# Layer 1's weighted sum moved next to the products of heads 0 to 3, and three PSUM places exchanged, in a two-layer graph attention kernel

## The chip, the cores and the metric

The kernel runs on one core of one Trainium2 chip. The metric is the device time in microseconds of one execution. A core has TensorE (PE in the profile, with its weight loads shown as PEld), VectorE (DVE), ScalarE (ACT), GpSimd (POOL) and SyncE (SP, which here only issues DMAs). Each engine runs its own instructions strictly in their order; between engines they wait for each other with semaphores.

## What is computed

There are 16 graphs of 1024 nodes with 256 features, and an adjacency matrix for each. Two layers are applied, each to normalised and rectified features, with a residual:

```
h = relu(layernorm(x))
x = x + L0(h, adj)      # 8 heads of 32: softmax(mask(Q K^T / sqrt(32))) V, then Wo
h = relu(layernorm(x))
x = x + L1(h, adj)      # scores by edge kind:
    e_k   = leaky_relu((h * a_k) h^T)         # k = 0..3
    score = e_k where adj == k + 1, else -9e15
    out   = softmax(score) h
```

With the inputs given, `adj` holds 0 and 1 only, so layer 1 needs `e_0` alone; the kernel checks this while it runs and has another path for more kinds, which is not taken here.

## The kernel before

A tile is 128 rows of one graph, so there are 128 tiles (`s` from 0 to 127, graph `b = s // 8`, tile `t = s % 8`). The main loop (line 839) runs over the tiles, and each turn of it, a *step*, has eight *places* `h` = 0 to 7, one for each head. The order in which instructions are issued is written out by hand in the loop's body, and each engine keeps to it. A step works on several tiles at once:

- `now` is the tile whose heads are computed. At place h: `scores(h)` (PE, L461), `softmax_max(h)` (DVE, L473), the exponential of the head before (`softmax_exp`, ACT, L490), and the transposition of the head before that: on the PE with a copy by ACT (`turn`, L590 and L591), or, for heads 0, 1, 4 and 5 in most tiles, as blocks on DVE with DMAs issued by SP (`turn_blocks`, `place_blocks`, L381 and L386). In tiles with t = 7 the heads 4 and 5 go by the PE too, and in tiles with t = 0 the heads 0 and 1.
- `combine(0)`, at place 7, multiplies heads 0 to 3 with the values; `combine(1)`, at place 3 of the next step, heads 4 to 7 (both L526, 64 matmuls each as the profile counts them, two for each that the code issues; their weights are 32 columns wide, and four of them lie side by side in the array).
- `was` is the tile before. It gets its reciprocals of the softmax sums (`turned_reciprocals`, ACT, L520, tile `recT`), `combined` (DVE, L536), the output product (`output`, PE, L541), the residual (`residual`, DVE, L547) and its norms (`norms`: DVE, then POOL).
- `piece` is the tile nine ahead, whose layer 0 inputs are made: `normed` (ACT, L223, tile `h`), `turn` (PE, two transposes, L237), `turned` (ACT, two copies, L249 and L250, tiles `hT` and `hTm`), k's projection `project(0, .)` (PE, L267 with `wkT`, eight matmuls of the profile), `raised(0)` (ACT, L309), `halve(0)` (POOL, next step). q's projection and the values follow in places 1 and 2 of the next step.
- `edge` is a tile of layer 1 (nine behind): scores in places 0 and 2, `softmax_max` at 3, `softmax_exp` (L680) at 6. `edge_was` is the layer 1 tile before. It gets its transposition at place 0, and its weighted sum `gather` (PE, L698): 64 matmuls of the profile in two halves of 32, each with weights 32 columns wide and 256 columns of data. `store` (DVE, L705 and L707, then a DMA that SP issues, L708) divides, adds the residual and writes the output.

Steps 10 to 127 have an `edge_was`, steps up to 118 a `piece`. Before step 10 there is no layer 1 tile to sum; after the loop eight layer 1 tiles are left and are done by a loop of their own (line 988).

PSUM places. Two banks hold four small places of 128x256 each (line 95): the first bank `sums_place` and `brief`, the second `early` and `late`. Before the change `sums_place` takes the products of `combine` and the sums of `gather`; `brief` the reciprocals and the transposed layer 1 nodes; `early` q's projection; `late` the transposed `h`, k's projection, the values and the output product. The scores have two larger places, `sides`: heads 4 and 6 and the layer 1 scores use the second, the other heads the first. The scores of a head can start when `softmax_max` has read what stood in its place.

The part of the loop that matters runs like this on the PE in an ordinary step (places 4 to 7 and the next 0): `scores(4)`, `turn(2)`, `output`, `scores(5)`, `turn(3)`, `gather(0)`, `piece.turn`, `scores(6)`, `gather(1)`, `project(0)`, `scores(7)`, `combine(0)`, `scores(0)`. On ACT, from place 3 on: `recT`, the layer 1 `bend` (L665), the kept layer 1 blocks (L647), `flag` of the next tile (L453), the exponential of head 3, two copies of head 2's transposes, `raised(1)` (L309), `normed` (L223), the exponential of head 4, two copies of head 3, `hT`, `hTm`, the exponential of head 5, the layer 1 exponential, the exponential of head 6, `raised(0)`.

Of the kernel before, what the change touches and what calls it, by code (L numbers as in the profile page):

```python
# [17 lines left out]
P = 128  # L18
# [12 lines left out]
def by_blocks(t):  # L31
    return BY_BLOCKS.get(t, MIXED)
# [15 lines left out]
def gnn_kernel(  # L48
# [46 lines left out]
    sums_place, brief, early, late = (banks[i // 2][:, i % 2, :] for i in range(4))  # L95
# [92 lines left out]
    class Piece:  # L188
# [66 lines left out]
        def project(self, which, oc):  # L255
            wT, bias = ((weights["wkT"], bk_t), (weights["wqT"], bq_t))[which]
            b, w = self.b, self.n * P
            if b not in kds:
                kds[b] = dram.tile([NC, P, 2, N], F32, tag="kd", name=f"kd_{b}")
            if b not in qds and which == 1:  # L260
                qds[b] = dram.tile([NT, NC, P, 2, 2, P], F32, tag="qd", name=f"qd_{b}")
            if self.n > 1:
                ps = ps_tr.tile([P, w], F32, tag="tr", name="proj")
            else:
                ps = (late, early)[which][:, oc * P : (oc + 1) * P]
            for fc in range(NC):
                nc.tensor.matmul(  # L267
                    ps,
                    lhsT=wT[:, fc, oc * P : (oc + 1) * P],
                    rhs=(self.hT, self.hTm)[which][:, fc, :],  # L270
                    start=(fc == 0),
                    stop=(fc == NC - 1),
                )

            self.projected.append((which, oc, ps, bias))
# [139 lines left out]
    class Attend:  # L415
# [120 lines left out]
            nc.vector.tensor_tensor(self.oT, by_chunk(sums_place), self.recT, ALU.mult)  # L536

        def output(self):
            self.y = late
            for g in range(NC):  # L540
                nc.tensor.matmul(  # L541
                    self.y, lhsT=self.oT[:, g, :], rhs=weights["woT"][:, g, :], start=(g == 0), stop=(g == NC - 1)
                )
# [50 lines left out]
    class Edges:  # L594


        def __init__(self, b, t, last=False):
            self.b, self.t, self.last = b, t, last
            self.rows = slice(t * P, (t + 1) * P)
            self.side = sides[t % 2 if last else 1]  # L600
            self.tags = {"sel": ("p", 4), "pT1": ("pT", 7)} if last else {}
            if last and t % 2:
                self.tags |= {"ha": ("hT", 1), "x1b": ("x1", 1), "h0": ("xb", 1)}
            self.sums = late if last and t % 2 else sums_place

        def buffer(self, tag, shape):
            tag, bufs = self.tags.get(tag, (tag, 1))
# [168 lines left out]
    def attend_of(s):  # L776
        return Attend(*divmod(s, NT)) if 0 <= s < B * NT else None
# [9 lines left out]
    with tc.manual_schedule():  # L787
        first = [Piece(0, 0, 4), Piece(0, 4, 4)]
        piece_was, piece_next = Piece(1, 0), piece_of(0)
        now, nxt = attend_of(0), attend_of(1)  # L790
# [39 lines left out]
        piece, edge, edge_was = piece_next, None, None  # L830
# [8 lines left out]
        for s in range(B * NT + 1):  # L839
            b, t = divmod(s, NT)  # L840

            def load_keys(h, end):
                if t == NT - 1 and b + 1 < B and 2 * h + end in KEY_STEPS:
                    load_key(b + 1, KEY_STEPS.index(2 * h + end))
                if t == 0 and 0 < b < B and 2 * (HEADS + h) + end in KEY_STEPS:
                    load_key(b, KEY_STEPS.index(2 * (HEADS + h) + end))

            nxt2, edge_nxt, piece_nxt = attend_of(s + 2), edges_of(s + 1), piece_of(s + 1)
            for h in range(HEADS):
                ending, eh = (now, h - 1) if h >= 1 else (was, HEADS - 1)  # L850
                turning, th = (now, h - 2) if h >= 2 else (was, HEADS + h - 2)

                load_keys(h, 0)


                if now:
                    now.scores(h)
                if h == 0 and piece_was:
                    piece_was.halve(0)
                if s == 0 and h == 1:  # L860
                    first[1].values()
                if h == 3 and edge:
                    edge.softmax_max()
                if h == 5:
                    if was:
                        was.residual()
                    norms(was, piece_nxt)
                if h == 6 and edge_was:
                    edge_was.gather(1)
                if now:  # L870
                    now.softmax_max(h)
                if h == 6 and edge_was:
                    edge_was.store()


                if h == 1 and edge:
                    edge.keep(0)
                if h == 2 and gone:
                    gone.turned_normed()
                if ending:  # L880
                    ending.softmax_exp(eh)

                if h == 3 and was:
                    was.turned_reciprocals()
                if h == 3 and edge:
                    edge.bend()
                    edge.keep(1)


                if h == 3:  # L890
                    if was:
                        was.combine(1)
                    if piece_was:
                        piece_was.biased()
                    if was:
                        was.combined()
                if turning and th in by_blocks(turning.t):
                    turning.turn_blocks(th)
                    turning.place_blocks(th)
                elif turning:  # L900
                    turning.turn(th, 0)
                    turning.turn(th, 1)


                if h == 0:
                    if edge:
                        edge.score(0)
                    if gone:
                        gone.normed()
                    if edge_was:  # L910
                        edge_was.turn_blocks()
                        edge_was.place_blocks()
                if h == 1:
                    if gone:
                        gone.turn_normed()
                    if piece_was:
                        piece_was.project(1, 0)
                        piece_was.project(1, 1)
                    if was:
                        was.reciprocals()  # L920
                    if piece_nxt:
                        piece_nxt.load()
                if h == 2:
                    if edge:
                        edge.score(1)
                    if piece_was:
                        piece_was.values()
                    if was:
                        was.turn_reciprocals()
                        was.add_bias()  # L930
                if h == 3:
                    if nxt:
                        nxt.load_queries()
                    if edge:
                        edge.leak()
                    if edge_was:
                        edge_was.load_nodes()
                    if nxt:
                        nxt.flag()
                        nxt.mask()  # L940
                if h == 4:
                    if was:
                        was.output()
                    if piece_was:
                        piece_was.raised(1)
                        piece_was.halve(1)
                    if piece:
                        piece.normed()
                    if piece_was:
                        piece_was.write_queries()  # L950
                    if edge_nxt:
                        edge_nxt.prepare()
                    if nxt2:
                        nxt2.load()
                if h == 5:
                    if edge_was:
                        edge_was.gather(0)
                    if piece:
                        piece.turn()
                    if piece:  # L960
                        piece.turned()
                if h == 6:
                    if edge:
                        edge.softmax_exp()
                    if was:
                        was.keep()
                    if now:
                        now.load_nodes()
                    if piece:
                        piece.project(0, 0)  # L970
                        piece.project(0, 1)
                if h == 7:
                    if now:
                        now.combine(0)
                    if piece:
                        piece.raised(0)
                load_keys(h, 1)
            gone, was, now, nxt = was, now, nxt, nxt2
            edge_was, edge = edge, edge_nxt
            piece_was, piece = piece, piece_nxt  # L980
# [84 lines left out]
```

## Time and profile before

| what | value |
|---|---|
| median of 3 runs | 3068.4 us (3067.28 to 3073.23) |
| the profiled execution | 3076.4 us, its span 3074.5 us |
| granted TensorE clock, mean | 0.996 |
| ACT busy, share of the span | 86% |
| DVE busy | 82% |
| POOL busy | 71% |
| matmuls of `gather` (L698), 8192 | 496.9 us busy, mean 382 ns |
| matmuls of `combine` (L526), 16384 | 533.4 us busy, mean 275 ns |

The span is the time from the first to the last instruction on the chip. "Busy" of the PE counts matmuls that overlap in the array, so its share tells that the PE was seldom without work, not how well it was used. A row of the timeline merges instructions of one kind that follow each other: its start, the time from the first start to the last end, and in brackets how long the engine had been idle before and what ended that. The difference between the starts of two neighbouring rows of the PE is therefore what a group cost the PE in its place.

### The profile page before, as it was taken

What the parts mean: (1) busy time and instruction counts of PE and PEld (TensorE: products, weight loads), DVE (VectorE), ACT (ScalarE), POOL (GpSimd) and SP (SyncE); (2) the same over time, 40 slices, a digit from 0 to 9 for tenths busy, and PEclk for the clock granted to TensorE, in tenths of its full rate; (3) what the DMA queues carried; (4) which work ended last, traced back from release to release, by engine and by line L of the source; (5) the groups of instructions that cost most, each with busy time, mean ns of one, the idle gap of its engine ahead of it and who ended that gap; (6) DMA issues with size and microseconds to landing.
All of it is one profiled execution on the core that took longest, in us unless ns stands there. A gap on an engine that the chain in (4) does not pass through costs nothing. (4 is left out here: it accounts for less than half of the span.)

```text
span 3074.5 us, 96254 instructions
## 1 busy us (share of the span) xinstructions
PE 2965.6 (96%) x36722; PEld 2230.1 (73%) x36722; DVE 2515.6 (82%) x4453; ACT 2654.5 (86%) x5159; POOL 2177.6 (71%) x2999
## 2 busy tenths in 40 slices
PE   7889999999999999999999999999999999999998
PEld 5667777777777777777777777777777777776664
DVE  5878888888888888888888788888888888888885
ACT  5888888899898998889889888988989888898882
POOL 3657777777777777777777777777777777776542
PEclk9999999999999999999999999999999999999999
DMA  7766777877777786777777777787777777777653
GB/s 245 219 219 205 237 235 222 255 216 243 231 225 243 230 257 209 232 247 220 246 230 228 235 232 243 221 255 221 220 247 228 251 211 235 237 227 236 191 168 100
DMA packets 597828, 695.68 MB, mean 226 GB/s; under 512 B 63280, under 2 KB 528560, under 8 KB 597360
## 3 DMA queue, kind: packets, MB, share of 16 engines
q1 hardware_dynamic: 528288, 477.29, 51.9%
q0 software_dynamic: 66960, 210.04, 21.0%
q8 instruction: 295, 4.83, 0.7%
q10 hardware_dynamic: 2112, 2.10, 0.2%
q14 instruction: 173, 1.42, 0.1%
HBM read 252.98 MB, written 134.22 MB: 126 GB/s over the span
## 5 line engine op out<-in xcount | busy, mean ns | idle before, releaser
L473 DVE CUSTOM_DVE_ANT_0 p<-s,neg 128x1024 f32<-128x1024 f32 x1024 | 1236.2, 1208 | 220.7 <-PE s L461 185.1
L490 ACT ACTIVATE p<-p,nmx 128x1024 f32<-128x1024 f32 x1024 | 1249.4, 1224 | 132.5 <-DVE nmx L473 123.9
L461 PE MATMUL s<-k,qt 128*128 128x512 f32 x2048 | 760.6, 453 | 15.5 <-DVE nmx L473 4.3
L591 ACT COPY pT<-trp 128x512 f32<-128x512 f32 x1024 | 549.4, 590 | 95.3 <-PE trp L590 94.9
L590 PE MATMUL trp<-ident,p 128*128 128x128 f32 x4608 | 604.5, 274 | 4.7 <-ACT pT L591 1.5
L590 PEld LDWEIGHTS trp<-ident,p 128*128 128x128 f32 x4608 | 531.0, 140 | 104.0 <-ACT pT L591 10.8
L381 DVE STREAM_TRANSPOSE blocks<-p 128x1024 f32<-128x1024 f32 x456 | 564.5, 1238 | 12.3 <-ACT p L680 10.6
L526 PE MATMUL acc<-pT,v 128*32 128x128 f32 x16384 | 533.4, 275 | 41.8 <-ACT recT L520 30.0
L526 PEld LDWEIGHTS acc<-pT,v 128*32 128x32 f32 x16384 | 453.5, 110 | 153.0 <-ACT recT L520 85.0
L698 PE MATMUL acc<-h,pT 128*32 128x256 f32 x8192 | 496.9, 382 | 2.8 <-DVE h L707 1.7
L441 POOL TENSOR_SCALAR neg<-adj 128x1024 bf16<-128x1024 int32 x128 | 467.9, 3655 | 42.9 <-ACT neg L453 33.7
L461 PEld LDWEIGHTS s<-k,qt 128*128 128x128 f32 x2048 | 322.9, 191 | 106.3 <-issue 43.0
L698 PEld LDWEIGHTS acc<-h,pT 128*32 128x32 f32 x8192 | 241.8, 109 | 207.8 <-issue 65.6
L676 POOL TENSOR_TENSOR sel<-sel,less 128x1024 f32<-128x1024 f32 x120 | 286.8, 2390 | 68.9 <-ACT less L665 47.6
L633 PE MATMUL s<-h1T,ha 128*128 128x512 f32 (+2 forms) x744 | 272.8, 490 | 2.7 <-ACT h1T L569 1.6
L674 POOL TENSOR_SCALAR less<-top 128x1 f32<-128x1 f32 x120 | 31.9, 266 | 274.0 <-DVE top L656 273.9
L324 POOL DMA_DIRECT2D qd<-halves x240 | 177.5, 780 | 58.7 <-POOL halves L314 31.8
L490 ACT ACTIVATION_READ_ACCUMULATOR p<-p,nmx 128x1 f32 x1024 | 206.8, 202 | 0.0
L510 POOL COPY wide<-rec 128x256 f32<-128x256 f32 x128 | 53.8, 420 | 204.2 <-DVE rec L508 204.2
L330 POOL DMA_DIRECT2D kd<-halves x240 | 172.2, 766 | 35.5 <-POOL halves L314 35.4
L314 POOL TENSOR_TENSOR halves<-full,halves 128x256 fp32r<-128x256 f32 x240 | 176.8, 737 | 20.6
L633 PEld LDWEIGHTS s<-h1T,ha 128*128 128x128 f32 x744 | 126.7, 190 | 70.7 <-issue 45.0
(117 smaller groups left out, 4328.4 us busy)
## 6 DMA issues: line engine op xcount, KB each, us to landing
pT<-blocks SPq DMA_DIRECT2D x2304, 128.0 KB, 3.5
qt<-qd SPq DMA_DIRECT2D x128, 512.0 KB, 4.5
k<-kd SPq DMA_DIRECT2D x128, 512.0 KB, 7.3
adj<-in_adj POOLq DMA_DIRECT2D x127, 512.0 KB, 5.0
qd<-halves POOLq DMA_DIRECT2D x240, 256.0 KB, 2.7
kd<-halves POOLq DMA_DIRECT2D x240, 128.0 KB, 4.1
xb<-in_x POOLq DMA_DIRECT2D x128, 128.0 KB, 4.2
x1d<-x SPq DMA_DIRECT2D x128, 128.0 KB, 4.0
```

The costliest lines, as they stand in the source:

```text
L324: nc.gpsimd.dma_start(out=qds[self.b][self.first, oc].rearrange("p u w n -> p u (w n)"), in_=halves.unsqueeze(1).to_broadcast([P, 2, 2 * P]),)
L381: nc.vector.transpose(blocks.rearrange("p b j q -> p j b q"), p)
L441: nc.gpsimd.tensor_scalar(self.neg, self.adj, 0.0, MASKED, ALU.is_equal, ALU.mult)
L461: nc.tensor.matmul(self.ps[:, cols], lhsT=self.qt[:, h, :], rhs=keysets[self.b][h][:, cols], start=True, stop=True,)
L473: nc.vector.tensor_tensor_reduce(out=p, in0=sides[h in self.second], in1=self.neg, scale=-SCALE, scalar=FLOOR, op0=ALU.add, op1=ALU.min, a ...
L490: nc.scalar.activation(to, of, AF.Exp, bias=nmx, scale=-1.0, accum_out=self.sums[:, h : h + 1])
L526: nc.tensor.matmul(sums_place[r * HD : (r + 1) * HD, g * P : (g + 1) * P], lhsT=vs[self.b][:, j, place_of(h) : place_of(h) + HD], rhs=self ...
L590: nc.tensor.transpose(tr[:, j, :], p[:, jj * P : (jj + 1) * P], ident)
L591: copy(pT[:, half * 4 : half * 4 + 4, :], tr)
L633: nc.tensor.matmul(self.side[:, cols], lhsT=self.ha[:, c, :], rhs=h1T[:, c, cols], start=(c == 0), stop=(c == NC - 1),)
L676: nc.gpsimd.tensor_tensor(self.sel, self.sel, self.less, ALU.subtract)
L698: nc.tensor.matmul(self.sums[a * HD : (a + 1) * HD, :], lhsT=self.pT[:, j, a], rhs=h1s[self.b][:, j, :], start=(j == 0), stop=(j == NT - 1),)
```

## The change

- k's projection goes to `brief` and the output product too; both were in `late`.
- The sums of `gather` go to `early` in the main loop; they were in `sums_place`. The tail's places stay as they were.
- At place 5, `softmax_max(5)` is issued before `residual` and `norms`, no longer after them. (At place 6 and the other places the order of `softmax_max` against the rest is as before.)
- `gather(0)` leaves place 5 and `gather(1)` place 6. Both come at place 7, with `store` behind them, ahead of `combine(0)`.
- `project(0, 0)` and `project(0, 1)` leave place 6 and come at place 7, behind `scores(7)` and what `turn` there is, ahead of `gather(0)`.
- `raised(0)` is issued ahead of `combine(0)`, no longer behind it.

```
-                ps = (late, early)[which][:, oc * P : (oc + 1) * P]
+                ps = (brief, early)[which][:, oc * P : (oc + 1) * P]
...
-            self.y = late
+            self.y = brief
...
-            self.sums = late if last and t % 2 else sums_place
+            self.sums = (late if t % 2 else sums_place) if last else early
...
                 if h == 3 and edge:
                     edge.softmax_max()
+                if now:
+                    now.softmax_max(h)
                 if h == 5:
                     if was:
                         was.residual()
                     norms(was, piece_nxt)
-                if h == 6 and edge_was:
-                    edge_was.gather(1)
-                if now:
-                    now.softmax_max(h)
-                if h == 6 and edge_was:
-                    edge_was.store()
...
                 if h == 5:
-                    if edge_was:
-                        edge_was.gather(0)
                     if piece:
                         piece.turn()
...
+                if h == 7:
                     if piece:
                         piece.project(0, 0)
                         piece.project(0, 1)
-                if h == 7:
+                    if edge_was:
+                        edge_was.gather(0)
+                        edge_was.gather(1)
+                        edge_was.store()
+                    if piece:
+                        piece.raised(0)
                     if now:
                         now.combine(0)
-                    if piece:
-                        piece.raised(0)
```

## The prediction

> **What bounds the kernel now.** I read the busy shares first, then the waits of the PE in the steady part, then one step's timeline on the PE and on ACT.
>
> ```profile
> PE 2965.6 (96%) x36722; PEld 2230.1 (73%) x36722; DVE 2515.6 (82%) x4453; ACT 2654.5 (86%) x5159; POOL 2177.6 (71%) x2999
> ```
>
> ```profile
> PE acc L526 <- ACT recT L520: 12.6, 27, 0.7
> PE acc L526 <- DMA pT<-blocks: 10.7, 15, 1.6
> PE s L633 <- ACT h1T L569: 1.1, 7, 0.2
> PE s L461 <- DVE nmx L473: 0.2, 1, 0.2
> ```
>
> The second fence is all that the PE's matmuls waited for between 260 and 2800 us: 25 us of 2540. In the steady part the PE is the bound, and a step is as long as the PE's rows put end to end. An ordinary step on the PE, with "..." where its places 0 to 2 follow or rows don't matter:
>
> ```profile
> 1432.81 0.81 PE L461 MATMUL s<-k,qt 128*128 128x512 f32 x2
> 1433.46 1.03 PE L590 MATMUL trp<-ident,p 128*128 128x128 f32 x8
> 1434.43 1.93 PE L698 MATMUL acc<-h,pT 128*32 128x256 f32 x32
> 1436.30 0.44 PE L237 MATMUL acc<-ident,h 128*128 128x128 f32 x2
> 1436.49 0.71 PE L461 MATMUL s<-k,qt 128*128 128x512 f32 x2
> 1437.13 1.93 PE L698 MATMUL acc<-h,pT 128*32 128x256 f32 x32
> 1439.00 1.16 PE L267 MATMUL acc<-hT,wkT 128*128 128x128 f32 x8
> 1439.91 0.72 PE L461 MATMUL s<-k,qt 128*128 128x512 f32 x2
> 1440.56 1.96 PE L526 MATMUL acc<-pT,v 128*32 128x128 f32 x64
> 1442.44 0.73 PE L461 MATMUL s<-k,qt 128*128 128x512 f32 x2
> ```
>
> The same stretch on ACT, from the step's `recT` on:
>
> ```profile
> 1428.18 0.37 ACT L520 COPY recT<-acc 128x256 f32<-128x256 f32 x1 [0.25 <-PE acc L516]
> 1428.91 1.06 ACT L665 ACTIVATE less<-sel 128x1024 f32<-128x1024 f32 x1 [0.35 <-DVE top L656]
> ...
> 1434.07 0.62 ACT L223 ACTIVATE h<-xin,shift,r 128x256 f32<-128x256 f32 x1
> ...
> 1436.77 0.37 ACT L249 COPY hT<-acc 128x256 f32<-128x256 f32 x1
> 1437.04 0.38 ACT L250 COPY hTm<-acc 128x256 f32<-128x256 f32 x1
> ```
>
> ACT works from 1428.18 to 1437.14 with one gap of 0.35 us. Its last product, `hT`, is what `project(0)` reads. The PE comes to `project(0)` only at 1439.00, because `gather(1)` stands before it: 1.86 us of cover. The next `recT` starts at 1450.63, so the step is 22.45 us.
>
> **The gain: fewer changes of the array's shape.** A `gather` half costs 1436.30 - 1434.43 = 1.87 us. Its 32 matmuls go in eight rounds of four; the first starts are spread over 1.93 - 0.38 = 1.55 us (0.38 is the mean of one), so a round is 1.55/7 = 0.22, and a half should cost 8 x 0.22 = 1.76. So leaving the 32-column shape costs 0.1; entering it costs another 0.1: `turn(3)` ahead of `gather` takes 0.97 (1434.43 - 1433.46) and 0.87 in other places, scores 0.64 against 0.57. The projection behind it takes 0.91, and 0.82 elsewhere. That is some 0.25 us for each stay in the shape. The change makes one stay of three (both halves and `combine(0)`): about 0.45 us a step less PE work.
>
> **What the moves cost on the path.** Once the PE is ahead, the step is a loop of two legs: ACT from `recT` to `hT`, then the PE from `project(0)` to the next `recT`. Before, 8.96 + 11.63 (1439.00 to 1450.63) = 20.59, that is 1.86 less than the step: slack. The change puts all of `gather`, which filled the time until `hT`, behind `project(0)`.
>
> - PE's way to `project(0)`: `turn(3)` from 1433.46 ends at 1434.33, `piece.turn` now waits for `h` (1434.69), so 1434.75 to 1434.95, `scores(6)` and `scores(7)` 2 x 0.58, so it stands at `project(0)` at 1436.1. ACT's order up to `hT` is unchanged, and all its inputs are there. The only time ACT can win is its 0.1 us wait for `piece.turn`, and I count none. `hT` is there at 1437.14. The PE waits 1 us.
> - From there: 0.05 for the semaphore, `project(0)` 0.91 + 0.09 for entering the shape, `gather` in one piece 16 x 0.22 = 3.5, `combine(0)` 1442.44 - 1440.56 = 1.88, and from `scores(0)` to `recT` as before 1450.63 - 1442.44 = 8.19. Sum 14.55; with ACT's 8.96 the loop is 23.5. An ordinary step gets 1.02 us longer. Other tiles have other mixes of layer 1 work, but 8.96 and 1.86 stay within 0.05 in most, so this holds for all with t below 7.
> - Steps with t = 7 have two more PE transposes, and their exponentials of heads 4 and 5 are slow:
>
> ```profile
> 1316.45 2.27 ACT L490 ACTIVATE p<-p,nmx 128x1024 f32<-128x1024 f32 x1
> ...
> 1320.03 2.25 ACT L490 ACTIVATE p<-p,nmx 128x1024 f32<-128x1024 f32 x1
> ```
>
>   `turn(5)` needs the second, and now stands ahead of `project(0)`. The exponential ends at 1322.2; 0.05 for the semaphore, `turn(5)` 0.87, projection 1.0, `gather` 3.5, `combine` 1.88: `scores(0)` at 1329.5, where it was at 1326.03. +3.5.
> - Steps 1 to 9 have no `gather`. Their trace already shows what `project(0)` does without cover:
>
> ```profile
> 102.59 1.16 PE L267 MATMUL acc<-hT,wkT 128*128 128x128 f32 x8 [1.64 <-ACT hTm L250]
> ```
>
>   There `combine(0)` will wait for `raised(0)`, which now stands ahead of it and reads the same bank. The changed program has that wait, as the old one has one of `combine(1)` on `recT`. `raised(0)` ends at 105.3, and `combine(0)` began at 104.14: +1.2.
> - In later steps that wait is covered: `raised(0)` ends 4.18 us after `hT` (1441.32), `combine(0)` starts 4.55 after. Were the cover gone, each 0.1 would cost 0.1 a step.
> - `softmax_max(5)` earlier costs the PE nothing; `scores(7)`, now right behind `scores(6)`, needs it by 1435.5. DVE is free at 1433.60 and needs 1.2 + 0.1. Queued behind it are `residual` and norms (0.42 to 1.65 us). `project(0)` needs the residual read out of `brief`, done by 1435.4; POOL takes up the norms at 1441.4. In the old order it would come 1.6 later and `scores(7)` wait 1.0, most of it inside the wait for `hT`.
> - `store` (0.64 us on DVE) now follows the last transposition at place 7, about 4.6 us after `hT`; DVE then has nothing until `scores(0)` at 6.5. Its output DMA on SP moves behind eight block DMAs; SP's next come after DVE's layer 1 transposition at place 0, later still. Both 0; without that gap 0.6 a step.
> - Exchanged places: every new reader (`residual`, `raised(0)`, `store`) is done before the next writer by the times above; 0.
> - Steps 119 to 127 have no `piece`: only the gain, -0.45.
>
> Steps 10 to 118 are 109, of which 13 have t = 7: 96 x 1.02 = 98, 13 x 3.5 = 45, 9 x 1.2 = 11, 9 x -0.45 = -4. Sum +150 us.
>
> **The clock.** In the first 260 us the granted clock falls to half seven times for 3.41 us, each time after a stretch in which the PE stood still half the time:
>
> ```profile
> 119.10:122.51 3.41, 1.73 (x11) 1.08 (x10) 3.19 (x8) 3.41 (x9) 2.93 (x5) 1.00 0.67 169
> 122.51:125.92 3.41, 3.41 (x30) 2.70 (x33) 2.56 (x4) 2.53 (x6) 2.95 (x8) 0.50 0.95 324
> ```
>
> (columns: window, length, busy PE, PEld, DVE, ACT, POOL, then the clock). A stretch with 1.89 busy did not set it off. In an ordinary changed step the PE would miss 0.3 + 1.0 in such a stretch, too little. With t = 7 it misses 1.6 (waiting for the first slow exponential) and 1.4 within 4.7 us: I give it an even chance, at up to 1.7 us, so 13 x 0.5 x 1.5 = 10 us. The Trainium skill's page "TensorE: Matmul & The Clock Gate" (HAM oscillation) puts the limit at idle gaps over about 3.4 us. By that rule nothing here would trip and 10 us would fall away; these rows show it with gaps of 1.64, and the rows decide.
>
> The profiled span becomes 3074.5 + 160 = 3234. The profiled run is 8 us above the median of the runs, so I name 3226.
>
> **Rivals.**
> - *The PE stays the bound* (faster): 118 steps x -0.45 = -53, so 3015. It needs `hT` 1.0 us sooner after `recT`; the break-even is an ACT leg of 7.95 in place of 8.96. For it: the PE has 96%, ACT only 86%. Against it: the leg is back to back but for a gap that DVE sets. 6 in 100.
> - *A smaller wait*: half of the 1.02, 3175 to 3060 as it shrinks. 2 in 100 for no change, 6 for a cost below 70 us.
> - *The clock halves in ordinary steps too*: up to 1.7 x 109 = 185 more, 3410. It decides once a 3.41 us stretch holds 1.7 us of idling, against 1.3 worked out. 8 in 100.
>
> **How the numbers follow.** Forecast 78 in 100, its own range 3180 to 3270 (ordinary steps at 0.7 to 1.3, t = 7 at 2.5 to 4.5). To reach the neighbouring cases I take 3120 to 3300. Measurements of this kernel tell 0.2% from no change. Faster 0.06, same 0.02, slower 0.92.
>
> **What would show it.** After: `L267` with `wkT` waiting for ACT's `hT` about 1 us in most steps, the matmuls' idle time up by some 100 to 200 us, `gather` one row of x64 in about 3.7, PE's share down to about 92%, steps of 23.5. Wrong, if steps are 22.0 and that wait is missing; wrong in size, if the clock drops throughout, or if `combine(0)` waits for `raised(0)` in late steps.

## The result, and the profile after

The changed kernel takes 3198.5 us (median of 4 runs, 3195.85 to 3199.1) where the kernel before, run beside it, takes 3070.2 (4 runs, 3067.28 to 3073.23). The ratio is 1.0416, 95% interval 1.0398 to 1.0434: slower, by 128 us between the medians. The profiled span went from 3074.5 to 3194.0 us, that is +119.5: the profiled run of the kernel before lay 8 us above the median on record ahead of the prediction, that of the changed kernel 2.7 below its own. The page's busy shares:

```profile
PE 2938.1 (92%) x36722; PEld 2269.7 (71%) x36722; DVE 2502.9 (78%) x4453; ACT 2623.2 (82%) x5159; POOL 2172.8 (68%) x2999
```

The busy times of PE, DVE, ACT and POOL are all a little lower than before, and their shares are lower still because the span grew. The time is therefore a new wait. The waits of the PE between 260 and 2900 us show which (engine, tile and line, then the releaser; total us, times, longest):

```profile
PE acc L267 <- ACT hT L249: 89.2, 95, 1.0
PE trp L590 <- ACT pT L591: 20.0, 13, 1.6
PE trp L590 <- ACT p L490: 19.0, 13, 1.5
PE acc L237 <- ACT h L223: 16.0, 63, 0.3
...
PE acc L526 <- ACT full L309: 3.0, 1, 3.0
```

The first row is new: in 95 steps `project(0)` stands still for `hT`, for 0.94 us in the mean. The second and third are new as well and come 13 times each: these are the steps with t = 7. The wait for `h` is on the way to the same place and costs nothing there, because the PE waits again two groups later. The 10.7 us of waits for block DMAs that stood in the same view of the kernel before have gone.

One ordinary step, first on the PE, then on ACT (the rows from one `recT` to the next; between them only the two that matter):

```profile
1496.18 0.44 PE L237 MATMUL acc<-ident,h 128*128 128x128 f32 x2 [0.23 <-ACT h L223]
1496.37 1.18 PE L461 MATMUL s<-k,qt 128*128 128x512 f32 x4
1498.54 1.16 PE L267 MATMUL acc<-hT,wkT 128*128 128x128 f32 x8 [0.99 <-ACT hT L249]
1499.63 3.66 PE L698 MATMUL acc<-h,pT 128*32 128x256 f32 x64
1503.11 1.93 PE L526 MATMUL acc<-pT,v 128*32 128x128 f32 x64
1504.96 0.73 PE L461 MATMUL s<-k,qt 128*128 128x512 f32 x2
```

```profile
1489.63 0.37 ACT L520 COPY recT<-acc 128x256 f32<-128x256 f32 x1 [0.26 <-PE acc L516]
...
1498.08 0.41 ACT L249 COPY hT<-acc 128x256 f32<-128x256 f32 x1
...
1502.01 0.65 ACT L309 ACTIVATE full<-acc,bk_t 128x128 f32<-128x128 f32 x2
...
1513.18 0.37 ACT L520 COPY recT<-acc 128x256 f32<-128x256 f32 x1 [0.26 <-PE acc L516]
```

ACT has `hT` done at 1498.49, 8.86 us after `recT`; `project(0)` starts at 1498.54, and the PE had been idle for 0.99 us. Behind it the whole weighted sum runs as one row of 64, and `combine(0)` follows without a pause. In the steps with t = 7, two waits stand in a row on the PE instead, and the projection comes only after the second:

```profile
1374.01 1.14 PE L590 MATMUL trp<-ident,p 128*128 128x128 f32 x8 [1.53 <-ACT pT L591]
...
1377.07 1.09 PE L590 MATMUL trp<-ident,p 128*128 128x128 f32 x8 [1.45 <-ACT p L490]
```

Measured from one `recT` to the next, the median step with t = 3 went from 22.45 to 23.55 us, with t = 7 from 25.23 to 28.44.

### The profile page after: what moved, and what is told of

The parts are those of the page before. It is cut to its first block, busy times and chain, and to the rows that moved or that the text cites. A ratio compares the mean times of both kernels' runs of the same rounds, so it can differ in the third digit from the quotient of the medians.

```text
span 3194.0 us, 95940 instructions
## 1 busy us (share of the span) xinstructions
PE 2938.1 (92%) x36722; PEld 2269.7 (71%) x36722; DVE 2502.9 (78%) x4453; ACT 2623.2 (82%) x5159; POOL 2172.8 (68%) x2999
## 3 DMA queue, kind: packets, MB, share of 16 engines
q0 software_dynamic: 66960, 210.04, 20.8%
## 5 line engine op out<-in xcount | busy, mean ns | idle before, releaser
L461 PE MATMUL s<-k,qt 128*128 128x512 f32 x2048 | 733.0, 447 | 12.9 <-DVE nmx L473 5.2
L526 PE MATMUL acc<-pT,v 128*32 128x128 f32 x16384 | 527.0, 275 | 49.2 <-ACT recT L520 30.2
L526 PEld LDWEIGHTS acc<-pT,v 128*32 128x32 f32 x16384 | 469.2, 110 | 130.1 <-ACT recT L520 85.2
L698 PE MATMUL acc<-h,pT 128*32 128x256 f32 x8192 | 473.5, 381 | 0.9 <-DMA pT<-blocks 0.5
L698 PEld LDWEIGHTS acc<-h,pT 128*32 128x32 f32 x8192 | 255.3, 110 | 178.8 <-DMA pT<-blocks 6.4
L267 PE MATMUL acc<-hT,wkT 128*128 128x128 f32 x960 | 137.6, 286 | 98.0 <-ACT hT L249 98.0
L490 ACT ACTIVATION_READ_ACCUMULATOR p<-p,nmx 128x1 f32 x1024 | 221.7, 217 | 0.0
L267 PEld LDWEIGHTS acc<-hT,wkT 128*128 128x128 f32 x960 | 116.2, 191 | 144.1 <-ACT hT L249 144.1
```

Of the source, the lines that this page charges most:

```text
L267: nc.tensor.matmul(ps, lhsT=wT[:, fc, oc * P : (oc + 1) * P], rhs=(self.hT, self.hTm)[which][:, fc, :], start=(fc == 0), stop=(fc == NC - 1),)
L461: nc.tensor.matmul(self.ps[:, cols], lhsT=self.qt[:, h, :], rhs=keysets[self.b][h][:, cols], start=True, stop=True,)
L490: nc.scalar.activation(to, of, AF.Exp, bias=nmx, scale=-1.0, accum_out=self.sums[:, h : h + 1])
L526: nc.tensor.matmul(sums_place[r * HD : (r + 1) * HD, g * P : (g + 1) * P], lhsT=vs[self.b][:, j, place_of(h) : place_of(h) + HD], rhs=self ...
L698: nc.tensor.matmul(self.sums[a * HD : (a + 1) * HD, :], lhsT=self.pT[:, j, a], rhs=h1s[self.b][:, j, :], start=(j == 0), stop=(j == NT - 1),)
```

## The experiments

The edits are shown against the changed kernel, those of 7 and 8 against the experiment before them; "..." marks what is left out. Step times are medians over steps 10 to 118.

**1. The projection behind the weighted sum.** If the 1 us is only a matter of who comes first, `gather` ahead of `project(0)` should cover it.

```
                 if h == 7:
-                    if piece:
-                        piece.project(0, 0)
-                        piece.project(0, 1)
                     if edge_was:
                         edge_was.gather(0)
                         edge_was.gather(1)
                         edge_was.store()
+                    if piece:
+                        piece.project(0, 0)
+                        piece.project(0, 1)
```

> The changed kernel with one move: project(0) goes behind both halves of gather (and ahead of raised(0) and combine(0)), so that gather covers the time until hT again. If the loss is only that project(0) waits about 1 us for ACT's hT, the wait vanishes and the time falls to 3010-3030 us. My theory says more: gather now writes early, in the bank of late, so it has to wait for hTm, ACT's last read of that bank, 0.3 us after hT; and combine(0) has to wait until raised(0) has read brief in its own bank, some 0.7 us after the projection, with nothing between them. An ordinary step then goes from 23.55 to about 24.4 us and the time to 3260-3320 us. A third theory, that the loss comes from one long stretch on the PE without scores, in which DVE and ACT run dry, expects no change: the stretch is as long as before (3190-3210 us).

Measured: 3368.2 us, ratio to the kernel before 1.0976 [1.0951, 1.1000]; the step with t = 3 takes 25.05, 1.50 more than in the changed kernel. The two waits are those expected, but the time is above the 3260 to 3320 named. The PE's timeline:

```profile
1500.80 3.66 PE L698 MATMUL acc<-h,pT 128*32 128x256 f32 x64 [1.26 <-ACT hTm L250]
1504.39 1.16 PE L267 MATMUL acc<-hT,wkT 128*128 128x128 f32 x8
1506.35 2.16 PE L526 MATMUL acc<-pT,v 128*32 128x128 f32 x64 [0.80 <-ACT full L309]
```

The sum does not need `hTm`, yet it waits for ACT to read it: its place `early` lies in the bank of `late`, where the transposed `h` stands. `combine(0)` then waits 0.80 us for `raised(0)`, which reads k's projection in `brief`, in the bank of `combine`'s own `sums_place`. This second wait is what was put too low: `combine(0)` starts 1.96 us after the projection (1506.35 - 1504.39) and then takes 2.08 until `scores(0)` in place of 1.85. In addition the clock falls to half in eight of the 13 steps with t = 7. So the new places tie the group to ACT whichever product comes first, and the order is not free. With these places the cover cannot be had back by exchanging the two alone.

**2. `hT` earlier on ACT.** The exponential of head 4 is issued behind the copies `hT` and `hTm`.

```
-                if ending:
+                if ending and not (h == 5 and piece):
                     ending.softmax_exp(eh)
...
                         piece.turned()
+                        if ending:
+                            ending.softmax_exp(eh)
```

> The changed kernel, with ACT's exponential of head 4 issued behind hT and hTm in place of ahead of the copies of head 3 (steps with a piece). hT comes 1.14 us earlier, which is more than the PE waits for it (0.99). My theory: the wait for hT vanishes in ordinary steps; then combine(0) comes 1 us earlier as well and meets raised(0), which ends where it did (4.2 us after the old hT), so a new wait of about 0.6 us appears there, and an ordinary step goes from 23.55 to about 23.15: 3155-3175 us. If nothing else is late, 22.55 a step and 3095-3110 us. If the long stretch without scores is the cause, no change: 3190-3210 us.

Measured: 3205.2 us, ratio 1.0442 [1.0420, 1.0465]. This expectation was missed. The wait for `hT` has gone, as it said, but the step with t = 3 is only 0.15 shorter (23.40). The PE's timeline shows what took its place:

```profile
1507.39 1.16 PE L267 MATMUL acc<-hT,wkT 128*128 128x128 f32 x8
...
1512.70 2.16 PE L526 MATMUL acc<-pT,v 128*32 128x128 f32 x64 [0.56 <-ACT full L309]
1514.79 0.73 PE L461 MATMUL s<-k,qt 128*128 128x512 f32 x2
```

`hT` comes 1.12 us sooner after `recT` (7.74 for 8.86), but `raised(0)` does not, since the exponential that stepped back stands ahead of it. From `project(0)` to `scores(0)` it is now 7.40 us (1514.79 - 1507.39) against 6.42 in the changed kernel: 0.98 of the 1.12 is given back, 0.56 as the wait for the bank and 0.42 because `combine(0)` no longer starts while `gather` ends and takes longer behind the wait. The expectation had the wait, but neither these 0.42 nor the clock. The steps with t = 7 got longer, 29.35 for 28.44, with a drop of the clock in each of them; the last section shows it.

**3. The same, with k's projection back in `late`.** If the bank is what gave it back, this takes the tie away.

```
-                ps = (brief, early)[which][:, oc * P : (oc + 1) * P]
+                ps = (late, early)[which][:, oc * P : (oc + 1) * P]
```

> e2 (ACT makes hT ahead of the exponential of head 4) with k's projection in late again, as before the change, so that combine(0) shares no bank with raised(0). In e2 the wait for hT had only gone over into one of combine(0) for raised(0) (0.56 us, and 0.24 more to take up the narrow shape after a pause). My theory: that wait goes, project(0) waits 0.2 us for hTm in its place, an ordinary step falls from 23.4 to 22.8 us, the t = 7 steps stay near 29.3: 3140-3165 us. If the shared bank has nothing to do with it, 3200-3210 us.

Measured: 3124.2 us, ratio 1.0170 [1.0151, 1.0189]. The step with t = 3 is 22.69, 0.71 less than in experiment 2, and the stretch is as long as in the changed kernel:

```profile
1479.81 1.16 PE L267 MATMUL acc<-hT,wkT 128*128 128x128 f32 x8
...
1484.38 1.93 PE L526 MATMUL acc<-pT,v 128*32 128x128 f32 x64
1486.24 0.73 PE L461 MATMUL s<-k,qt 128*128 128x512 f32 x2
```

6.43 us, and no wait of `combine(0)`. The total came lower than the 3140 to 3165 expected. The step is 0.1 shorter than named, and the first nine steps take 20.8 us less than in experiment 2: there they wait for `raised(0)` too, and half clock falls into nine windows of 3.41 us, here into two. Two waits are now told apart: `hT` on ACT, and `raised(0)` through the bank of `combine`.

**4. The steps with t = 7.** `project(0)` and `gather` go ahead of place 7's transposition, so that they fill the time of the slow exponential.

```
+                if h == 7:
+                    if piece:
+                        piece.project(0, 0)
+                        piece.project(0, 1)
+                    if edge_was:
+                        edge_was.gather(0)
+                        edge_was.gather(1)
                 if turning and th in by_blocks(turning.t):
                     turning.turn_blocks(th)
...
                 if h == 7:
-                    if piece:
-                        piece.project(0, 0)
-                        piece.project(0, 1)
                     if edge_was:
-                        edge_was.gather(0)
-                        edge_was.gather(1)
                         edge_was.store()
```

> The changed kernel, with project(0) and gather issued ahead of place 7's transposition. On the PE this differs only in the 13 steps with t = 7 that have a piece (and the two behind them): there turn(5), which waits for a slow exponential of 2.2 us, no longer stands ahead of the projection. My theory: these steps go from 28.45 to about 27.0 us, the others stay at 23.55: 3175-3185 us. If the 3.2 us that these steps lost come from something else than turn(5) and its place, nothing changes: 3195-3200 us.

Measured: 3184.7 us, ratio 1.0369 [1.0346, 1.0392]. Steps with t = 7 fall from 28.44 to 27.06, all others stay within 0.01. The second of the two t = 7 waits is what the edit removed; the first stays (19.9 us in 13 steps), and with it 1.83 of the 3.21 us that such a step had lost. In five of the 13 steps the clock falls to half, and they take 28.6.

**5. `softmax_max(5)` back behind the residual and norms.**

```
-                if now:
-                    now.softmax_max(h)
                 if h == 5:
                     if was:
                         was.residual()
                     norms(was, piece_nxt)
+                if now:
+                    now.softmax_max(h)
```

> The changed kernel with softmax_max(5) again behind residual and norms. By the prediction scores(7), which now follows scores(6) directly, then waits up to 1.0 us for it, nearly all of it inside the 1 us that project(0) waits for hT: 3195-3210 us. If the early softmax_max(5) is what holds the changed order together, its loss shows in full: some 1 us a step, 3290-3310 us.

Measured: 3209.1 us, ratio 1.0439 [1.0423, 1.0455], so 0.2 to 0.3% over the changed kernel; the two intervals overlap. Three steps with t = 7 at half clock, 2 us longer each, are part of it. The wait moves one group forward on the PE and `project(0)` then waits no longer:

```profile
1477.55 0.73 PE L461 MATMUL s<-k,qt 128*128 128x512 f32 x2 [0.92 <-DVE nmx L473]
1478.11 1.12 PE L267 MATMUL acc<-hT,wkT 128*128 128x128 f32 x8
```

The step with t = 3 is 23.55, as in the changed kernel. Of two waits in a row on an engine, the one that ends last decides; the other may be 0.92 us or nothing.

**6. The projection last.** The weighted sum goes ahead of place 7's transposition, `combine(0)` behind it, `project(0)` and `store` last; `raised(0)` moves to the next step's place 0 behind the exponential. `gather` sums in `brief`, k's projection goes to `early`.

```
-                ps = (brief, early)[which][:, oc * P : (oc + 1) * P]
+                ps = (early, early)[which][:, oc * P : (oc + 1) * P]
...
-            self.sums = (late if t % 2 else sums_place) if last else early
+            self.sums = (late if t % 2 else sums_place) if last else brief
...
+                if h == 0 and piece_was:
+                    piece_was.raised(0)
+                    piece_was.halve(0)
...
+                if h == 7 and edge_was:
+                    edge_was.gather(0)
+                    edge_was.gather(1)
                 if turning and th in by_blocks(turning.t):
...
                 if h == 7:
+                    if now:
+                        now.combine(0)
                     if piece:
                         piece.project(0, 0)
                         piece.project(0, 1)
                     if edge_was:
-                        edge_was.gather(0)
-                        edge_was.gather(1)
                         edge_was.store()
-                    if piece:
-                        piece.raised(0)
-                    if now:
-                        now.combine(0)
```

> The changed kernel with project(0) behind combine(0), gather ahead of place 7's transposition, store behind combine(0), raised(0) (and halve(0)) behind the exponential of head 7 in the next step; gather's sums go to brief and k's projection to early, so that no two that follow each other share a bank with a reader in between. PE work and the long stretch without scores (gather, combine, projection: 6.3 us) stay as in the changed kernel. My theory: hT and raised(0) are covered, the PE is the bound again with one stay in the narrow shape less than before the change, two less in ordinary steps: 22.0-22.2 a step, 3010-3040 us, faster than both kernels. If the long stretch without scores starves DVE and ACT, it is slower than before the change: 3100-3200 us.

Measured: 3055.7 us, ratio 0.9955 [0.9939, 0.9972]: 0.45% faster than the kernel before, but short of the 3010 to 3040 expected. The step with t = 3 is 22.29, but those with t = 7 are 27.04, which the expectation had not seen, and in half of all steps `piece.turn` waits some 0.3 us for `h` (17.0 us in 66 steps). Both waits in one step with t = 7:

```profile
1487.26 0.44 PE L237 MATMUL acc<-ident,h 128*128 128x128 f32 x2 [0.28 <-ACT h L223]
...
1489.70 1.14 PE L590 MATMUL trp<-ident,p 128*128 128x128 f32 x8 [1.52 <-ACT pT L591]
```

This run also tells against a rival reason for the loss: that a long stretch of the PE without scores starves DVE and ACT. The stretch of `gather`, `combine(0)` and `project(0)` is as long here, and the step is 1.26 shorter than in the changed kernel.

**7. And `piece.turn` one place later.** On top of 6, `piece.turn` and `piece.turned` move to place 6, and in steps with t = 7 `gather` comes at place 6 to cover the slow exponential.

```
-                if h == 7 and edge_was:
+                if h == (6 if t == NT - 1 else 7) and edge_was:
                     edge_was.gather(0)
                     edge_was.gather(1)
...
-                if h == 5:
+                if h == 6:
                     if piece:
                         piece.turn()
                         piece.turned()
```

> e6 with two more moves. piece.turn and turned go from place 5 to place 6 (the PE no longer waits 0.28 us for h), and in steps with t = 7 gather goes to place 6, behind scores(6), where it covers the slow exponential that turn(4) and turn(5) wait for. My theory: ordinary steps 22.0 in place of 22.3, t = 7 steps 25.0 in place of 27.0: 3000-3020 us, 1.6 to 2.2% faster than before. If the long stretch of the PE without scores costs something by itself, less: 3035-3055 us.

Measured: 3004.6 us, ratio 0.9778 [0.9765, 0.9791], the fastest version. The page's busy shares, the PE's longest waits between 260 and 2900 us, and a step's end on the PE:

```profile
PE 2895.5 (97%) x36722; PEld 2252.9 (75%) x36722; DVE 2506.8 (84%) x4453; ACT 2641.4 (88%) x5159; POOL 2172.7 (72%) x2999
```

```profile
PE acc L526 <- ACT recT L520: 18.2, 34, 1.6
PE acc L698 <- DVE x L547: 4.5, 14, 0.3
```

```profile
1445.46 3.66 PE L698 MATMUL acc<-h,pT 128*32 128x256 f32 x64
1448.94 1.93 PE L526 MATMUL acc<-pT,v 128*32 128x128 f32 x64
1450.80 1.16 PE L267 MATMUL acc<-hT,wkT 128*128 128x128 f32 x8
1451.72 0.70 PE L461 MATMUL s<-k,qt 128*128 128x512 f32 x2
```

The PE waits as little as before the change, and in ordinary steps `gather` and `combine(0)` make one stay in the 32-column shape in place of three. The step with t = 3 is 21.89: 0.56 under the kernel before.

**8. The gain alone.** As 7, but with `gather(0)` at place 6 and `gather(1)` at 7 in ordinary steps: two stays.

```
-                if h == (6 if t == NT - 1 else 7) and edge_was:
-                    edge_was.gather(0)
+                if h == 6 and edge_was:
+                    edge_was.gather(0)
+                if h == (6 if t == NT - 1 else 7) and edge_was:
                     edge_was.gather(1)
```

> e7 with gather(0) behind scores(6) and gather(1) behind scores(7) in ordinary steps, so the array goes into the narrow shape once more in each step, with the same matmuls and no new wait. It prices a stay. By the rows of before, 0.25 us: 118 steps without those of t = 7 and 0 make 25-30 us more than e7. If joining the halves is worth nothing, the same as e7.

Measured: 3058.0 us, ratio 0.9948 [0.9933, 0.9964]; the step with t = 3 is 22.52, 0.63 over experiment 7. That is twice what was expected, and the waits say why:

```profile
PE acc L698 <- DVE x L547: 36.5, 114, 0.4
```

36.5 / 114 = 0.32 us a step is a new wait of `gather(0)` for the residual, read out of `brief`, where the sums are to go. With it `gather(0)` starts 1.03 us after `scores(6)`, where scores ahead of `gather` take 0.64 without a wait (1437.13 - 1436.49 before the change):

```profile
1453.59 0.71 PE L461 MATMUL s<-k,qt 128*128 128x512 f32 x2
1454.62 1.93 PE L698 MATMUL acc<-h,pT 128*32 128x256 f32 x32 [0.32 <-DVE x L547]
```

So the wait costs 0.39 of the 0.63, and 0.24 is left for the second stay.

The exchange of places alone, without the moves, was not tried.

## Why the prediction was right

The forecast was 3226 us from a sum of +160 on the span; the median is 3198.5, and the span rose by 119.5. The mechanism is the one named: the weighted sum was the cover of `hT`, and without it the step is the loop of ACT up to `hT` and of the PE from `project(0)`.

**The ordinary step.** ACT's leg was put at 8.96 and is 8.86; the rest, from the end of `hT` to the next `recT`, was put at 14.55 and is 14.69 with t = 3 and 4; the step was put at 23.5 and is 23.55. There is a slip in the adding: the terms as printed make 14.62 and not 14.55, so the step should have read 23.58, 1.13 longer and not 1.02, and the whole sum some 10 us more. That the slip went towards the measured time is luck. The wait of about 1 us, the row of 64 in 3.66 and the PE's 92% stand in the profile as named. What moved the size is in the table (us on the profiled span; measured by steps from `recT` to `recT`).

| term | predicted | measured |
|---|---|---|
| steps with t = 2 to 6, 70 of them | 70 x 1.02 = 71 | 63.7 |
| steps with t = 0 and 1, 26 | 26 x 1.02 = 27 | 12.8 |
| steps with t = 7, 13 | 45 | 41.5 |
| clock, in t = 7 | 10 | 0 |
| start and first nine steps | 11 | 5.8 |
| last nine steps | -4 | -3.2 |
| after the loop | 0 | -1.1 |
| sum | 160 | 119.5 |

**The term that was most off** is "8.96 and 1.86 stay within 0.05 in most, so this holds for all with t below 7". In steps with t = 0 and 1 ACT's leg shrank from 10.02 to 9.17 and from 8.96 to 8.45, so they lost only 0.33 and 0.65 us. Before the change ACT waited there for the PE's `piece.turn`, which stood behind `gather(0)`. ACT's row for `hT` in a step with t = 1, in the kernel before and in the changed one:

```profile
812.04 0.37 ACT L249 COPY hT<-acc 128x256 f32<-128x256 f32 x1 [0.30 <-PE acc L237]
```

```profile
842.75 0.40 ACT L249 COPY hT<-acc 128x256 f32<-128x256 f32 x1
```

The prediction counted that wait as 0.1 and its removal as nothing. With t = 3 its 0.1 is just what ACT's leg lost; with t = 1 this row shows 0.30 of the 0.51, and with t = 0 a wait of 0.34 for the output product went besides the same 0.30:

```profile
784.74 0.63 ACT L309 ACTIVATE full<-acc,bq_t 128x128 f32<-128x128 f32 x2 [0.34 <-PE acc L541]
```

This is `raised(1)`, which reads `early`; the output product stood in `late`, in the same bank. The kernel before has 27 such waits, 8.5 us together, and the changed kernel, with the output product in `brief`, none. So the exchange of places, put at 0, also gained something.

**Steps with t = 2 to 6.** Their medians rose by 0.96 to 1.17, in the mean 1.08. 70 x 1.08 would be 76; the missing 12 us lie in some 14 steps of the kernel before that were longer than the others of their t, by up to 1.8 us each; 9.2 us of it are waits for block DMAs. In the changed kernel these steps are as long as the others. The sum made from one typical step could not see them.

**Steps with t = 7** were put at +3.5 and cost 3.2. Experiment 4 shows the named cause: with `turn(5)` behind the projection and the sum, 1.38 of it goes. The other wait, of `turn(4)`, was not in that term; the prediction had seen it only as idling for the clock. Once the later wait is gone, this one holds the step up, and only experiment 7, where `gather` fills both, comes back to 25.18.

**The clock** did not fall in these steps, where the prediction gave it an even chance. The idling was as it put it, two waits of 1.5 us, but no 3.41 us window of the steady part held more than 1.79 us of it. That it was none of 13 is chance: experiment 5, with the same two waits, has half clock in three of these steps. (For the first 260 us the prediction counts seven drops of 3.41 us; the trace of the kernel before has six.)

**The first steps** were put at 9 x 1.2. `combine(0)` does wait for `raised(0)` there, 16.0 us in 9 waits between 40 and 260 us. Steps 2 and 4, at full clock in both kernels, went from 19.72 and 19.62 to 20.65 and 20.66, so the wait cost 1.0 and not 1.2. The sum left out that `hT` also comes earlier: ACT's leg fell from about 8.57 to 8.18, most of it a wait of 0.29 for the output product, and with it `raised(0)` ends 11.23 us after `recT` in place of 11.63 (step 2). The rest is the clock, which the sum left out: half clock falls into five of these nine steps before the change and into two after it. Step 3, with one such window before, went from 21.18 down to 20.66.

**The gain of 0.25 for a stay** agrees in size: two stays fewer are worth 0.56 in experiment 7, and one more costs 0.24 in experiment 8 beyond its wait. In the changed kernel what is saved ahead of `project(0)` lies inside the new wait. The last nine steps, without a `piece`, got 3.2 us shorter in all, near the 4 of the sum, but by luck: seven of them gained 0.81 to 1.02 each, twice the 0.45, and the two with t = 7 lost 1.8 each, because the transpositions that wait for the slow exponentials stand ahead of `gather` there too. What else the seven gained stays open.

**The claims of zero.** Late steps hold the cover of `raised(0)`: one such wait in the changed kernel between 260 and 2900 us. Its margin of 0.4 was real, as experiment 2 overran it. `softmax_max(5)` in the old order costs 0.3% at most, as a wait that mostly hides in the one for `hT`. The exchange of places was called free; in the order of the change the late steps show no wait for it, but experiments 1 to 3 show that the new places make other orders dear. For `project(0)` the exchange was a gain: it starts 0.05 us after `hT` in the changed kernel and 0.33 after it in experiment 3, where k's projection is back in `late`.

## What to carry to other kernels

Before work is moved on an engine that runs in order, look at what stands behind it and when that thing's input is ready: work that seems only to fill time may be the cover of a late result, and the step then becomes the sum of the two engines' legs however busy each is. Grouping the products of one array shape went with a time 2.2% shorter once the late result was read last, not first (experiment 7; two stays fewer at 0.24 to 0.28 us are most of it), and with one 4.2% longer in the order of the change. When such a group is put together, place its accumulators so that no other engine still reads in the same PSUM bank: moving one tile to the other bank took a wait away that an earlier `hT` alone could not (experiments 2 and 3).

## What the runs showed of the hardware that was not expected

**When the clock halves.** In experiment 2 the idling of a t = 7 step lies in one piece of 2.63 us in place of two of 1.5. Three windows of such a step, with length, busy PE, granted clock, DMA share and GB/s:

```profile
1572.20:1575.60 3.40, 3.22 (x23) 1.00 0.81 246
1575.60:1579.00 3.40, 0.91 (x4) 1.00 0.86 258
1579.00:1582.40 3.40, 3.17 (x13) 0.50 0.96 283
```

The clock is halved for the stretch that follows the idle one, in all 13 of these steps, and each is 0.9 us longer than in the changed kernel. Experiment 3 prices a drop within one kernel: its steps with t = 7 take 28.7 us in the four cases without half clock, 29.4 to 29.8 in the six with one window of it, and 30.6 to 31.6 in the three with two.

In each profile the drops start at whole multiples of 3.413 us from one another. On that grid, over the ten profiles between 262 and 2900 us, no window at full clock with less than 1.74 us of idle PE was followed by half clock, and every one with more than 1.86 was. Before 262 us the border is less sharp: a window with 1.58 idle was followed by half clock (experiment 4, 39.73 to 43.14 us), and one with 1.90 was not (changed kernel, 105.70 to 109.11 us). Two pieces of 1.5 us, which the grid can cut apart, set it off in none of the 13 steps of the changed kernel and in three of experiment 5. The Trainium skill's page "TensorE: Matmul & The Clock Gate" (HAM oscillation) puts the limit at idle gaps over about 3.4 us. Here a gap of 2.63 was enough, and these rows decide.

**Some waits cost more than their length.** `combine(0)` without a pause takes 1.85 us until `scores(0)` starts (1504.96 - 1503.11 in the changed kernel) and 2.09 behind a wait (1514.79 - 1512.70 in experiment 2), 0.24 more. Not every wait adds this: in the kernel before, `combine(1)` takes 1.88 until the next group starts (1522.96 - 1521.08) behind a wait of 0.69 us for `recT`. What decides stays open.
